# A decoder layer on one core: the order of work at the change of halves, in the fourth block's sums, at the first experts and at the load of the output weights

## The chip, the cores and the metric

The kernel runs on one core of a Trainium2 chip. Its time is the device time of one execution in microseconds (us). A core has five engines that run side by side, each working through its own queue in order: TensorE (PE in the profile; the loads of its weights are PEld), VectorE (DVE), ScalarE (ACT), GpSimd (POOL) and SyncE (SP), which here issues most DMA transfers. An engine waits for another by a semaphore. All data are float32.

## The reference, cut to what matters

The input x has 32 sequences of 64 tokens with 512 features, so 2048 tokens. Three residual blocks follow each other, each behind a layer norm.

```python
x = x + attn(layernorm(x))      # 32 heads of 128, within each sequence
x = x + cross(layernorm(x), ctx_1024)
x = x + ffn(layernorm(x))       # 64 experts, 8 chosen

# attn
q = rmsnorm(h @ Wq + bq, gq); k = rmsnorm(h @ Wk + bk, gk); v = h @ Wv + bv
o = softmax(q @ k.T / sqrt(128)) @ v          # per sequence and head
return o @ Wo + bo

# ffn
scores = softmax(h @ router_weight.T + router_bias)
w = top 8 of scores, zero elsewhere
return h * w.sum() + w @ expert_bias
```

Most of the work is in the four large products with Wq, Wk, Wv (512 x 4096 each) and Wo (4096 x 512).

## The kernel before, in words

**Tokens.** The 2048 tokens are 16 tiles of 128, 8 pairs of tiles, 4 quads of 2 pairs, and 2 halves of 2 quads. The attention goes through half 0 with all 16 groups of two heads, then through half 1. The variable `n` counts the 32 steps; `n = 16` is the change of halves, `n = 17` the second step of half 1.

**Strassen-like block products.** A product with the weights is split into 2 x 2 blocks and done with seven block products instead of eight. The seven left factors of a pair of tiles are called by number: 1 is a11, 2 is a12, 4 is a22, and 5, 6, 7, 3 are the sums s1 = a21 + a22, s2 = s1 - a11, s3 = a11 - a21, s4 = a12 - s2. `AttentionInput` makes them: `turn_first` turns the first tile of the pair on TensorE (L273) and copies a11 and a12 out of PSUM (L364, L365); `turn_second` turns the second, copies a22 (L372) and makes the sums s3 (L375), s1 (L376), s2 (L378) and s4 (L383).

**The first step of a half** (`hg == 0`) is done by `single`, one unit (a quad) after the other. `HeadGroup.project` issues the block products for q and k in the order 1, 2, 6, 5, 7, 4, 3, with those of the values (L440, `values`) between them; where `fifth_ahead` is set, as for the first unit of all, 5 comes ahead of 6. Products 1, 6, 7 and 4 add up in one PSUM bank (`pa`), 5 and 3 in another (`pb`), 2 in a third (`pc`); VectorE reads a bank (L513, L518) before the next product may add to it. `single` runs other work at numbered places between the products: `between[2]` is the place after the first product of the values, and so on. The line "turned probabilities" (`line.turn`) is at place 7. At `n = 0` the turning of the next inputs is at places 7 and 12, at `n = 16` at 6 and 11.

**All other steps** are done by `double`: a `Window` computes two units at once, with the scheme applied a second time inside each block, so that there are 7 x 7 products (L717). Its left factors are the token sums of `inner_input`: for each of the seven blocks `o`, two sums on VectorE (L393, L394), then two on GpSimd (L396, L397). They are made in steps 0 and 1 of each half. `Window.project` goes through four groups of blocks, (1, 5), (2, 6), (7, 3) and (4), each in four parts; the dictionary `more` puts work behind part (n, m). Behind parts (2, 1) to (3, 2) the window itself adds up parts of q and k on GpSimd for its first unit and on VectorE for its second (`add`, L797), and takes squares of them on ScalarE (L407). ScalarE also copies the values out of their bank (`keep`, L456), and the next product of the values adds to that bank.

**What sets the order.** TensorE's order is the program's order. In the attention that of VectorE, ScalarE and GpSimd is too. SP's order, and in the tail (from the output product on) that of VectorE, ScalarE and GpSimd, is set by a planner from its own costs. So an edit of the program moves an instruction on TensorE for certain, and on SP only where the planner follows.

**The fetches.** Behind a window ScalarE writes the inverse roots of the mean squares to DRAM (row writes, L684), and SP fetches them back, spread over all partitions (`rs`, L595), for the scaling of q and k on GpSimd and VectorE (L604, L606).

**The output product** (L911) needs Wo in four quarters; `load_wo` loads them (L883), the first into a buffer that the last but one step's weights held, issued in the program ahead of the last window.

**The tail** runs the rest of the layer for each tile (`cross_attention`, then `experts`) piece by piece between the output products of the following pairs; a generator's `yield w` says how many steps of the output products to let pass. `experts` ends with two products with the expert biases, one for each tile (L1283), added to x on VectorE (L1285), and the store of the result. They, like the output products, take their PSUM banks from `ps_a`, which has three. The next x tiles are loaded into the buffers of those that were stored, and GpSimd adds the bias to them (L899).

Of the kernel before, what the change touches and what calls it, by code (L numbers as in the profile page):

```python
# [24 lines left out]
NPAIR = NT // 2  # L25
# [16 lines left out]
def decoder_layer(  # L42
# [23 lines left out]
    nc = tc.nc  # L66
# [143 lines left out]
    first = const.tile([P, 1], F32, tag="first", name="first")  # L210
# [96 lines left out]
    class AttentionInput:  # L307
# [39 lines left out]
        def turn_first(self, copy=None, pool=None, tag="ps"):  # L347
            copy = copy or nc.scalar.copy
            pair = self.pair
            self.turned(pool or ps_s, tag)  # L350
            half, t, j = pair // 4, pair // 2 % 2, pair % 2
            if pair % 4 == 0:


                halves_x[half] = {o: block(f"x{o}_{half}") for o in (1, 2, 6, 5, 7, 3, 4)}
            raw = {
                o: it[:, 0 : 8 * P].rearrange("p (c t j n) -> p c t j n", c=2, t=2, j=2)
                for o, it in halves_x[half].items()
            }
            if j == 0:  # L360
                quads[pair // 2] = {o: it[:, :, t, :, :] for o, it in raw.items()}
            self.parts = [raw[o][:, :, t, j, :] for o in range(1, 8)]
            a11, a12 = self.parts[0:2]
            copy(a11, self.pt[0][:, 0:2, :])  # L364
            copy(a12, self.pt[0][:, 2:4, :])  # L365

        def turn_second(self):
            pair = self.pair
            self.turned(ps_s, "ps")
            pt = self.pt  # L370
            a11, a12, s4, a22, s1, s2, s3 = self.parts
            nc.scalar.copy(a22, pt[1][:, 2:4, :])  # L372
            first = pair < 2
            if not first:
                nc.vector.tensor_tensor(s3, a11, pt[1][:, 0:2, :], ALU.subtract)  # L375
            nc.vector.tensor_tensor(s1, pt[1][:, 0:2, :], a22, ALU.add)  # L376
            yield
            (nc.vector if first else nc.gpsimd).tensor_tensor(s2, s1, a11, ALU.subtract)  # L378
            yield
            if first:  # L380
                nc.vector.tensor_tensor(s3, a11, pt[1][:, 0:2, :], ALU.subtract)
                yield
            nc.gpsimd.tensor_tensor(s4, a12, s2, ALU.subtract)  # L383
            if pair in (NPAIR // 2, NPAIR // 2 + 1):
                coming.append(AttentionInput(pair + 2))

    inner_x = {}

# [824 lines left out]
    def experts(t, xt):  # L1213
        name = f"f{t}"
        xn = layernorm(xt, name)
        yield 3
        if t % 2 == 0:
            fts = work.tile([P, 2, KC, P], F32, tag="att", name=f"ft_{name}", bufs=1)
        else:
            fts, x_a, xn_a = chosen_by.pop(t - 1)  # L1220
        ft = fts[:, t % 2, :, :]
        nc.scalar.copy(ft, transposed(xn.rearrange("p (kc k) -> p kc k", k=P), name))
        yield 1
        if t % 2 == 0:
            chosen_by[t] = fts, xt, xn
            return
        tiles = [(t - 1, x_a, xn_a), (t, xt, xn)]

        plt = ps_s.tile([P, P], F32, tag="ps", name=f"plt_{name}")
        for kc in range(KC):  # L1230
            for side in range(2):
                nc.tensor.matmul(
                    plt[side * NEXP : (side + 1) * NEXP, :],
                    rwt[:, kc, :],
                    fts[:, side, kc, :],
                    start=kc == 0,
                    stop=kc == KC - 1,
                )
        lgt = work.tile([P, P], F32, tag="wt", name=f"lgt_{name}")
        nc.scalar.copy(lgt, plt)  # L1240
        yield 0
        pl = ps_s.tile([P, 2, NEXP], F32, tag="ps", name=f"pl_{name}")
        nc.tensor.transpose(pl.rearrange("p a e -> p (a e)"), lgt, ident)
        n = len(tiles)
        lgs = work.tile([P, n, NEXP], F32, tag="lg", name=f"lg_{name}")
        nc.vector.tensor_tensor(
            lgs, pl, rb_b.unsqueeze(1).to_broadcast([P, n, NEXP]), ALU.add
        )
        wds = work.tile([P, n, NEXP], F32, tag="wds", name=f"wds_{name}")
        for side, (at, x_, xn_) in enumerate(tiles):  # L1250
            lg = lgs[:, side, :]
            top = small.tile([P, 8], F32, tag="top", name=f"top{side}_{name}")
            nc.vector.max(top, lg)
            neg = small.tile([P, 1], F32, tag="neg", name=f"neg{side}_{name}")
            nc.vector.tensor_scalar(neg, top[:, 0:1], -1.0, None, ALU.mult)
            ex = work.tile([P, NEXP], F32, tag="ex", name=f"ex{side}_{name}")
            den = small.tile([P, 1], F32, tag="den", name=f"den{side}_{name}")
            nc.scalar.activation(ex, lg, AF.Exp, bias=neg, accum_out=den)
            inv = small.tile([P, 1], F32, tag="inv1", name=f"inv1{side}_{name}")
            nc.vector.reciprocal(inv, den)  # L1260

            rest = work.tile([P, NEXP], F32, tag="rest", name=f"rest{side}_{name}")
            nc.vector.match_replace(rest, top, lg, -3e38)
            chosen = work.tile([P, NEXP], F32, tag="chosen", name=f"chosen{side}_{name}")
            nc.vector.tensor_tensor(chosen, lg, rest, ALU.not_equal)
            wd = wds[:, side, :]
            nc.vector.scalar_tensor_tensor(wd, ex, inv, chosen, ALU.mult, ALU.mult)
            ws = small.tile([P, 1], F32, tag="ws", name=f"ws{side}_{name}")
            nc.vector.tensor_reduce(ws, wd, AX.X, ALU.add)

            nc.vector.scalar_tensor_tensor(x_, xn_, ws, x_, ALU.mult, ALU.add)
        yield 2
        n *= NEXP
        pw = ps_t.tile([P, P], F32, tag="pt", name=f"pw_{name}")
        nc.tensor.transpose(pw[0:n, :], wds.rearrange("p a e -> p (a e)")[:, 0:n], ident)
        wt = work.tile([P, P], F32, tag="wt", name=f"wt_{name}")
        nc.scalar.copy(wt[0:n, :], pw[0:n, :])
        yield 1

        pms = [ps_a.tile([P, D], F32, tag="pa", name=f"pm{i}_{name}") for i in range(len(tiles))]  # L1280
        for i, pm in enumerate(pms):
            rows = slice(i * NEXP, (i + 1) * NEXP)
            nc.tensor.matmul(pm, wt[rows, :], eb_sb[rows, :], start=True, stop=True)  # L1283
        for (at, it, _), pm in zip(tiles, pms):
            nc.vector.tensor_tensor(it, it, pm, ALU.add)  # L1285
            nc.sync.dma_start(out=out_flat[bass.ts(at, P), :], in_=it)
# [178 lines left out]
    coming = []  # L1465
# [141 lines left out]
    for n, (hg, half) in enumerate(groups):  # L1607
        w = weights.pop(n)
        units = [HeadGroup(hg, 2 * half + t, w) for t in range(2)]
        prepare(n)  # L1610
        if hg == 0:
# [4 lines left out]
            }  # L1616
            if n > 0:
                half_two = [coming.pop(0).turn_second() for _ in range(2)]
                between[2] = lambda: [list(it) for it in half_two]
            else:  # L1620

                rest = [it.turn_second() for it in first_two]
                between[1] = lambda: w_0.one_sum(nc.vector, 5)
                between[2] = lambda: (
                    [next(it) for _ in range(2) for it in rest],
                    w_0.one_sum(nc.vector, 6),
                    [next(it) for it in rest],
                )
                between[4] = lambda: (
                    w_0.one_sum(nc.gpsimd, 4),  # L1630
                    w_0.one_sum(nc.gpsimd, 7),
                    [next(it, None) for it in rest],
                )
                for at in (11, 6):
                    between[at + 1] = between.pop(at)
                units[0].fifth_ahead = True
# [26 lines left out]
        else:  # L1663
# [7 lines left out]
            def also(n, m, it):  # L1671
                more.setdefault((n, m), []).append(it)

            if hg == 1:
                for at, o in (
                    ((0, 0), 2),
                    ((0, 1), 6),
                    ((0, 1), 3),
                    ((1, 0), 7),
                    ((1, 1), 3),  # L1680
                    ((1, 2), 4),
                    ((2, 2), 4),
                ):
                    also(*at, lambda o=o: inner(o))
            if half == 0 and 2 <= hg < 2 + NT // 2:
# [12 lines left out]

            if n + 1 == len(groups):
                four = four_blocks("wo_0")  # L1700
                wo_b = [[load_wo(0, 0, four[0:2], nc.sync)], []]
                also(1, 0, lambda: wo_b[1].append(load_wo(1, 0, four[2:4], nc.scalar)))
                a_0 = [[None, None], [None, None]]

# [84 lines left out]
    a12 = drain()  # L1789
# [110 lines left out]
```

## Time and profile before

| | us |
|---|---|
| median of 3 runs | 1857.03 |
| runs | 1856.47 to 1858.2 |
| the profiled execution | 1858.04 |
| its span (first to last instruction) | 1856.3 |
| TensorE busy | 1840.5 |
| GpSimd busy | 1009.6 |
| VectorE busy | 1248.4 |

The granted clock of TensorE was 1.00. In the timeline a row has the start of a group of equal instructions in us from the span's start, the time from its start to its end in us, engine, line, operation, what is written and what is read, shapes and count. In brackets behind it stand the idle time of the engine just before, and what ended it. The view of waits has: who waited at which line, for whom; us in total, how often, the longest. A matmul here is recorded as two, and its recorded duration reaches over the start of the next, since matmuls overlap; 128x256 ones start 0.216 us apart.

### The profile page before, as it was taken

The page shows a single profiled execution, that of the slowest core. Times are in us where ns is not written, and L with a number is a line of the kernel's source. Part 1 is how long each engine was busy: PE and PEld are TensorE (multiplying, and loading weights), DVE is VectorE, ACT ScalarE, POOL GpSimd, SP SyncE. Part 2 cuts the span into 40 slices and gives each one's busy share as a digit, 9 for nine tenths or more (in the row PEclk, how much of TensorE's full clock was granted, in tenths as well). Part 3 has the DMA queues.
Part 4 walks back from the last instruction along what each step waited for, and adds up shares of the span by engine and source line. Part 5 has one row for each costly group of instructions (what it writes and reads, how often), then busy time and mean ns, then how long its engine had stood idle before and what let it go on. Part 6 is the DMA issues. An engine that isn't in the chain of part 4 may idle for free.

```text
span 1856.3 us, 40645 instructions
## 1 busy us (share of the span) xinstructions
PE 1840.5 (99%) x16892; PEld 1606.4 (87%) x16892; DVE 1248.4 (67%) x2112; ACT 653.3 (35%) x1583; POOL 1009.6 (54%) x850
## 2 busy tenths in 40 slices
PE   9999999999999999999999999999999999999998
PEld 8889889998899888899889988988888788888876
DVE  7767787776677768777677777777684444544455
ACT  3343444344433443434443344344412112211222
POOL 4966777776667639777666776776242211211120
PEclk9999999999999999999999999999999999999999
DMA  4244434433443343333344333333945221233100
GB/s 143 70 138 148 127 122 131 126 109 117 131 132 115 115 138 115 104 115 103 117 133 129 115 115 109 110 104 123 297 134 193 94 102 61 83 105 109 54 26 23
DMA packets 164937, 215.06 MB, mean 116 GB/s; under 512 B 10192, under 2 KB 135696, under 8 KB 160656
## 3 DMA queue, kind: packets, MB, share of 16 engines
q1 hardware_dynamic: 157648, 206.36, 34.6%
q10 hardware_dynamic: 7104, 6.10, 1.0%
q8 instruction: 133, 2.18, 0.5%
q14 instruction: 52, 0.43, 0.1%
HBM read 172.05 MB, written 40.37 MB: 114 GB/s over the span
## 4 chain that ended last, share of the span: by engine, by line
PE 90%; DVE 3%; DMA 3%; POOL 3%; issue 1%; ACT 0%; SPq 0%; DVEq 0%; POOLq 0%; ACTq 0%
PE p_w L717 33%; PE py L911 20%; PE va L440 11%; PE vb L440 8%; PE o L654 3%; PE s L617 3%; PE ms_w L853 3%; PE pt_p L273 1%; PE pa L498 1%; PE e_x L1140 1%; PE py_x L1156 1%; PE pt_x L273 1%; POOL w L133 1%; DMA wo<-in_wo_dram 1%; PE py_x L1151 1%
## 5 line engine op out<-in xcount | busy, mean ns | idle before, releaser
L717 PE MATMUL p_w<-x,w 128*128 128x256 f32 x2940 | 721.4, 382 | 3.7 <-POOL x L396 1.6
L717 PEld LDWEIGHTS p_w<-x,w 128*128 128x128 f32 x2940 | 522.2, 191 | 60.0 <-POOL x L396 1.8
L440 PEld LDWEIGHTS va<-w,x 128*128 128x128 f32 x2048 | 268.6, 192 | 13.1 <-issue 0.3
L728 DVE TENSOR_TENSOR qk<-p_w,qk 128x512 f32<-128x512 f32 x360 | 213.4, 600 | 93.9 <-PE p_w L717 90.7
L456 ACT COPY v<-va 128x256 f32<-128x256 f32 x256 | 96.0, 375 | 496.5 <-PE va L440 496.5
L440 PE MATMUL va<-w,x 128*128 128x128 f32 x2048 | 270.0, 275 | 0.0
L741 DVE TENSOR_TENSOR qk<-p_w,qk 128x512 f32<-128x512 f32 x360 | 219.9, 620 | 41.1 <-PE p_w L717 37.7
L133 POOL TENSOR_TENSOR w<-w 128x768 f32<-128x768 f32 x124 | 244.3, 1982 | 2.4
L289 POOL TENSOR_TENSOR prob<-prob,inv 128x512 f32<-128x512 f32 x64 | 79.7, 1246 | 296.1 <-DVE inv L288 280.0
L604 POOL TENSOR_TENSOR qk<-qk,rs 128x512 f32<-128x512 f32 x128 | 174.2, 1361 | 115.4 <-DMA rs<-row_w 105.3
L911 PE MATMUL py<-wo,a 128*128 128x256 f32 x992 | 227.1, 382 | 0.0
L407 ACT ACTIVATE sq<-qk 128x512 f32<-128x512 f32 x256 | 161.4, 631 | 181.5 <-DVE qk L741 65.9
L911 PEld LDWEIGHTS py<-wo,a 128*128 128x128 f32 x992 | 184.1, 190 | 33.2 <-issue 8.9
L440 PEld LDWEIGHTS vb<-w,x 128*128 128x128 f32 x1536 | 201.5, 192 | 9.6
L440 PE MATMUL vb<-w,x 128*128 128x128 f32 x1536 | 202.4, 275 | 0.0
L606 DVE SCALAR_TENSOR_TENSOR qk<-qk,gqk,rs 128x512 f32<-128x512 f32 x128 | 175.6, 1372 | 5.0 <-DMA rs<-row_w 5.0
L911 PE MATMUL py<-wo_t,a 128*128 128x256 f32 x672 | 155.0, 382 | 0.0
L911 PEld LDWEIGHTS py<-wo_t,a 128*128 128x128 f32 x672 | 124.8, 190 | 19.2 <-issue 2.4
L1035 POOL TENSOR_TENSOR x<-x,p 128x256 f32<-128x256 f32 x42 | 40.7, 991 | 163.1 <-ACT p L1088 73.3
L460 DVE TENSOR_TENSOR v<-vb,v 128x256 f32<-128x256 f32 x192 | 80.9, 421 | 55.5 <-ACT v L456 29.4
L797 POOL TENSOR_TENSOR qk<-qk 128x256 f32<-128x256 f32 x120 | 102.9, 858 | 10.6 <-DVE qk L741 5.8
L281 DVE TENSOR_REDUCE mx<-s 128x8 f32<-128x512 f32 x64 | 44.1, 690 | 86.0 <-PE s L617 86.0
(253 smaller groups left out, 2228.3 us busy)
## 6 DMA issues: line engine op xcount, KB each, us to landing
rs<-row_w SPq DMA_DIRECT2D x120, 512.0 KB
mixed<-ot SPq DMA_DIRECT2D x64, 512.0 KB
a<-mixed SPq DMA_DIRECT2D x32, 1024.0 KB
w<-in_wq_dram SPq DMA_DIRECT2D x64, 256.0 KB
w<-in_wk_dram SPq DMA_DIRECT2D x62, 256.0 KB
w<-in_wv_dram SPq DMA_DIRECT2D x62, 256.0 KB
x<-in_x_dram SPq DMA_DIRECT2D x20, 256.0 KB
rs<-row SPq DMA_DIRECT2D x8, 512.0 KB
```

The costliest lines, as they stand in the source:

```text
L133: on.tensor_tensor(*(it.rearrange("p c j d -> p (c j) d") for it in (out, a, b)), ALU.subtract)
L407: nc.scalar.activation(sq, of, AF.Square)
L440: nc.tensor.matmul(to[:, j, :], left[i][:, c, j, :], right[i][:, c, 2, :], start=first and j == 0 and c == 0, stop=c == 1, skip_group_chec ...
L456: nc.scalar.copy(self.v[h, ab], what)
L460: nc.vector.tensor_tensor(it, what, it, ALU.add)
L604: nc.gpsimd.tensor_tensor(k, k, rk, ALU.mult)
L606: lambda: nc.vector.scalar_tensor_tensor(q, q, gqk, rq, ALU.mult, ALU.mult)
L717: nc.tensor.matmul(bank[:, s, :], self.w.inner[o][i], inner_x[self.half, o][i], start=first and s == 0, stop=True, skip_group_check=True,)
L728: nc.vector.tensor_tensor(to(t, j), bank, add(t, j), ALU.add)
L741: nc.vector.tensor_tensor(to(t, j), bank, to(t, j), ALU.add)
L797: on.tensor_tensor(to, to, what, ALU.add)
L911: nc.tensor.matmul(py, a[:, g, :], b[g // KH][:, g % KH, :], start=n == 0 and g == 0, stop=n == last and g == NHG - 1,)
```

## The change

It has five parts.

1. In `turn_first` the copy of a12 is always made by ScalarE; where pairs 4 and 5 are turned ahead of half 1, VectorE made it.
2. For pairs 4 and 5 `turn_second` now works as it did for pairs 0 and 1: s1 first, then s2 on VectorE instead of GpSimd, then s3, with s4 alone left to GpSimd; three steps at place 2 of the unit, the last at place 4. The loads of the following pairs are asked for at its beginning. The first unit of half 1 takes product 5 ahead of product 6.
3. The GpSimd sums of block 4 (L396, L397) go from behind part (2, 2) of the window to behind part (2, 0), in both halves.
4. The first pair of tiles' expert products (t = 1) come one step sooner.
5. The first load of the output weights goes from ahead of the last window to behind its part (0, 3), in the program.

```diff
             copy(a11, self.pt[0][:, 0:2, :])
-            copy(a12, self.pt[0][:, 2:4, :])
+            nc.scalar.copy(a12, self.pt[0][:, 2:4, :])
...
-            first = pair < 2
+            first = pair % 4 < 2
+            if pair in (NPAIR // 2, NPAIR // 2 + 1):
+                coming.append(AttentionInput(pair + 2))
...
             nc.gpsimd.tensor_tensor(s4, a12, s2, ALU.subtract)
-            if pair in (NPAIR // 2, NPAIR // 2 + 1):
-                coming.append(AttentionInput(pair + 2))
...
-        yield 1
+        yield 0 if t == 1 else 1
         pms = [ps_a.tile([P, D], F32, tag="pa", name=f"pm{i}_{name}") for i in range(len(tiles))]
...
                 half_two = [coming.pop(0).turn_second() for _ in range(2)]
-                between[2] = lambda: [list(it) for it in half_two]
+                between[2] = lambda: [next(it) for _ in range(3) for it in half_two]
+                between[4] = lambda: [next(it, None) for it in half_two]
+                units[0].fifth_ahead = True
...
-                    ((2, 2), 4),
+                    ((2, 0), 4),
...
-                wo_b = [[load_wo(0, 0, four[0:2], nc.sync)], []]
+                wo_b = [[], []]
+                also(0, 3, lambda: wo_b[0].append(load_wo(0, 0, four[0:2], nc.sync)))
```

## The prediction

> **What bounds the kernel now.** I read the page first, then the waits of TensorE, then the timeline of each place where it waits.
>
> ```profile
> PE 1840.5 (99%) x16892; PEld 1606.4 (87%) x16892; DVE 1248.4 (67%) x2112; ACT 653.3 (35%) x1583; POOL 1009.6 (54%) x850
> ```
>
> TensorE is busy for 99% of a span of 1856.3 us and the change removes no matmul. So it can win only idle time of TensorE, about 16 us, start and end included. The view of waits names it:
>
> ```profile
> PE s L617 <- POOL qk L604: 1.9, 3, 1.1
> PE p_w L717 <- POOL x L396: 1.6, 1, 1.6
> ...
> PE p_w L717 <- DVE qk L728: 1.3, 1, 1.3
> PE pm_f L1283 <- DVE x L1285: 0.8, 1, 0.8
> ...
> PE pa L498 <- DVE x L364: 0.7, 1, 0.7
> ...
> PE pa L498 <- POOL x L378: 0.6, 1, 0.6
> ```
>
> Five of these rows are what the change touches: L364 and L378 (change of halves), L396 (token sums of the fourth block), L1285 (first experts) and L728 (which waits for a fetch beside the first load of the output weights). Measured from one matmul's start to the next, less the usual spacing, they cost 0.91, 0.79, 1.74, about 1.0 and 1.50 us. All of it together is 5.9 us or 0.32%. The question is which wait comes next at each place.
>
> **1. Change of halves.** TensorE and then VectorE:
>
> ```profile
> 672.41 2.00 PE L498 MATMUL pa<-x,w 128*128 128x256 f32 x8 [0.74 <-DVE x L364]
> ...
> 679.41 2.00 PE L498 MATMUL pa<-x,w 128*128 128x256 f32 x8 [0.62 <-POOL x L378]
> ...
> 684.73 0.60 PE L273 MATMUL pt_p<-ident,prob 128*128 128x128 f32 x4
> 685.17 1.89 PE L498 MATMUL pa<-x,w 128*128 128x256 f32 x8
> ```
> ```profile
> 681.44 0.69 DVE L513 TENSOR_TENSOR qk<-pa,bqk 128x512 f32<-128x512 f32 x1 [2.19 <-PE pa L498]
> ```
>
> (a) Two of four copies go from VectorE to ScalarE. The first product needs the third of the old four (671.94 to 672.35). It can now run as soon as its transposes end at 671.66, so at 671.70 to 672.12: product one starts 0.24 us sooner. The moved copies stand behind ScalarE's store of the mixture, which ends at 673.13. They end at about 673.7, and the second product needs them at 675.76: hidden by the first product, the values and the transposes.
>
> (b) Product six waited for s2 on GpSimd. Product five, which needs only s1 (VectorE, by 676.8), takes its place, so the 0.79 us go: it starts at 678.38. s2 is now on VectorE: two operations of 0.42 us where GpSimd's were 0.73. VectorE has six operations before the sum for product two instead of four, and that sum ends at about 678.9. Its square waits a little, and TensorE doesn't wait for it. s4 is done by 679 and is needed at 690.
>
> (c) What is late next: products six and seven write the same bank, and VectorE must read six (L513, 0.69 us) before seven may add to it. Before, the values, a transpose and product five (together 3.5 us) lay between. Now only the turned probabilities do (0.44 us). In the first half the same reordering moves the turning of the next inputs to this place; here that is not done. By the rows: six starts at 681.87 and ends at 683.76; VectorE then takes 0.03 + 0.69 us; seven starts at 684.53 instead of 684.04, and a restart costs 0.10 more. After seven TensorE stands at 686.36 where it stood at 686.90. Net of (a) to (c): **0.54 us won** of 1.70. Bounds: 0.3 (if VectorE is late with pair six's sums) and 1.03 (if seven doesn't wait).
>
> (d) On SP the fourth of the coming inputs falls behind two fetches, about 1 us later. Its transposes are at 690.4, more than 10 us after, so it is hidden. The two fetches gain 0.4 us or so; who waits for them (GpSimd's and VectorE's scaling) is not waited for by TensorE here.
>
> **2. Fourth block's token sums.** TensorE, GpSimd, ScalarE in the second half:
>
> ```profile
> 752.90 1.05 PE L440 MATMUL va<-w,x 128*128 128x128 f32 x8
> 755.52 1.13 PE L717 MATMUL p_w<-x,w 128*128 128x256 f32 x4 [1.57 <-POOL x L396]
> 756.49 1.05 PE L440 MATMUL va<-w,x 128*128 128x128 f32 x8
> ```
> ```profile
> 751.28 3.33 POOL L797 TENSOR_TENSOR qk<-qk 128x256 f32<-128x256 f32 x4
> 754.57 0.91 POOL L396 TENSOR_TENSOR x<-x 128x256 f32<-128x256 f32 x1
> 755.55 0.73 POOL L397 TENSOR_TENSOR x<-x 128x256 f32<-128x256 f32 x1
> ```
> ```profile
> 753.84 0.63 ACT L407 ACTIVATE sq<-qk 128x512 f32<-128x512 f32 x1 [3.19 <-POOL qk L797]
> 754.64 0.63 ACT L407 ACTIVATE sq<-qk 128x512 f32<-128x512 f32 x1 [0.17 <-POOL qk L797]
> 755.18 0.35 ACT L456 COPY v<-va 128x256 f32<-128x256 f32 x1
> ```
>
> GpSimd is full: it ran without a gap from 741.7. The change puts L396 and L397 ahead of the four L797 in the same queue, so the six end where they ended, at about 756.2, and it is the L797 that are late, by 1.65 us. Two chains hang on them. The second L797 releases VectorE's L728 (0.42 us), which frees the bank for product six: 754.5 + 0.42 gives 755.0, against 755.52. So this wait shrinks only by 0.5 us. The third and fourth release two squares on ScalarE, and behind these, in its queue, stands the copy L456 of the values. In the row above that copy starts at 755.18 although the matmuls it reads ended at 753.95. The next value product (756.49) may not write before it has read. After the change: fourth L797 ends 756.15, second square starts 756.18, copy 0.54 us later (755.18 less 754.64), 0.35 to 0.37 us long, then 0.05: the value product starts at 757.12 instead of 756.49. With a restart of 0.07 that is **0.70 us lost**, not 1.74 won. Bounds: 1.74 won (if the copy is not held up), 1.0 lost (if the L797 take the 0.9 us that the slowest took).
>
> A rule bears on this. The Trainium skill, SBUF — State Buffer, section Who interferes with whom: a VectorE instruction with two inputs in SBUF and a GpSimd one that reads it exclude each other, and the later one blocks fully. The rows show less: L797 on GpSimd took 0.91 us beside VectorE's own L797 and 0.73 alone, though a full block until 751.60 would have added 0.32. The moved L396 and L397 now stand beside those two VectorE sums. By the rows the loss is 0.70; with full blocks about 0.2 more, 0.90. I take the rows.
>
> First half: at the same place GpSimd has slack (L396 ended 86.17, needed 87.01), so nothing is there to win. Moved ahead, the fourth L797 ends at 86.9 instead of 85.2, the copy at 87.86 instead of 87.58, and the value product at 87.88 waits to 87.91: **0.1 us lost** with its restart, bounds 0 and 0.3.
>
> **3. First experts.**
>
> ```profile
> 1473.33 1.12 PE L1283 MATMUL pm_f<-eb_sb,wt_f 64*128 64x512 f32 x2
> 1475.23 1.12 PE L1283 MATMUL pm_f<-eb_sb,wt_f 64*128 64x512 f32 x2 [0.78 <-DVE x L1285]
> ```
>
> The second product takes the bank of the first, because the two before it are still held by output products whose sums come later on VectorE. Moved four output matmuls and the energies ahead (to 1470.3), the pair keeps that order: first product, VectorE's sum (0.69 us; VectorE idles there too), second product. The weights are ready at 1468.52. The wait moves and stays: 0. What follows is sooner or hidden: the stores and the next two x loads start some 3.5 us earlier; the energies and their softmax come 3 us later, ready near 1480 with their transposes at 1486.31. Bounds: 0.9 won, 0.3 lost.
>
> **4. Output weights.** SP's queue is not in the program's order; a planner sets it. In the compiled order of both kernels the two loads stand at the same place: behind the mixture's store, ahead of the row writes and all four fetches. So nothing moves, and the 1.50 us stay. It is 0.
>
> **Sum.** -0.54 + 0.70 + 0.10 + 0 + 0 = **+0.26 us** on the profiled span of 1856.3, with 1.74 us around it (1858.04). That execution lies 1.0 us above the median of 1857.03; the difference put on the median gives **1857.3 us**.
>
> **Rivals.**
> - *The sums' wait really goes.* If the squares on ScalarE do not hold the copy, -0.54 - 1.74 gives 1854.8 us. For it: the view of waits names L396 alone. Against: three queues in order, shown above.
> - *All that is named is won*, 0.91 + 0.79 + 1.74 + 0.9 = 4.3 us, 1852.7; with the fetch too, 1851.2. Against: steps 1c, 3 and 4.
> - *Slower: VectorE is held at the first experts.* Its compiled order now has the sum L1079 ahead of the two softmax normalisations. It waits for GpSimd's L899, which waits for an x load (row: landed 2.65 us after its issue at 1477.87). Issued near 1474.1 it lands near 1476.8 and holds nothing. From a landing past 1482 (8 us) the transposes at 1486.31 are late, us for us; 3.7 us lost needs a landing near 1486. Then 1861 us.
> - *No part does anything* gives 1857.0, inside the forecast.
>
> **Chances.** The forecast 0.72 (own range 1856.3 to 1858.3), the first rival 0.16, the second 0.05, the third 0.07. 0.2% is 3.7 us, about what a measurement of this kernel can tell from no change. Faster by more: 0.06 (second rival and a little of the first). Slower by more: 0.03, as the third rival mostly stays below that. Within: 0.91. The range runs from near the first rival to the forecast with its losses at their bounds and a run's scatter of 0.9 us: 1854.9 to 1858.9.
>
> **What would show it.** Right: before the second product seven at the change of halves a wait of about 0.4 us for L513; no wait for L396, but one of about 1.1 us of the value product for the copy L456 near 757; 0.8 us at the experts and 1.3 us at L728 unchanged. Wrong: squares before which GpSimd is done by 754.7, or a wait of VectorE for L899 that TensorE feels.

## The result: 2.8 us slower, less than two parts in a thousand

| | median | lowest to highest | runs |
|---|---|---|---|
| before | 1855.59 us | 1853.96 to 1858.2 | 18 |
| after | 1858.54 us | 1856.7 to 1861.01 | 18 |

The ratio is 1.0015, with an interval from 1.0008 to 1.0022: 1.5 to 4.1 us slower. The forecast of 1857.3 us stood for +0.26 us. That the change would move the time by less than 0.2% was right (the interval just reaches 0.22%); the small loss is real and ten times the forecast, and most of it came from a place that the forecast did not look at.

The profiled execution after took 1859.26 us, its span is 1857.4 us. The page's first part, as before, shows an engine that is never short of work:

```profile
PE 1839.4 (99%) x16892; PEld 1605.3 (86%) x16892; DVE 1244.6 (67%) x2112; ACT 653.8 (35%) x1585; POOL 1007.8 (54%) x848
```

The waits of TensorE after (what waited, for what; us in total, times, longest):

```profile
PE p_w L717 <- DVE qk L728: 3.9, 4, 1.6
...
PE e_x L1140 <- ACT prob_x L1186: 1.4, 1, 1.4
PE va L440 <- ACT v L456: 0.8, 1, 0.8
PE pm_f L1284 <- DVE x L1286: 0.8, 1, 0.8
...
PE pa L498 <- DVE x L364: 0.5, 1, 0.5
...
PE pa L498 <- DVE qk L513: 0.3, 1, 0.3
```

The waits for L378 and for L396 are gone. New are L513 (0.3) and L456 (0.8), which the forecast named, L728 at the window of the fourth block's sums (one of the four), and a wait of the energies' product L1140 for a softmax (1.4), which it did not. To see where time is lost and won I laid TensorE's start times of the two profiles side by side, matmul by matmul, and noted where the difference steps:

| place (us after) | step | what |
|---|---|---|
| 672 to 686 | -0.51 | change of halves |
| 755 to 757 | +0.68 | token sums, second half |
| 88 | +0.19 | token sums, first half |
| 1468 to 1476 | -0.40 | first experts |
| 1785 to 1788 | +1.89 | the last pair of cross attention: L1140 waits for the softmax L1186 |
| up to 22 | -1.17 | the first loads |
| 111 to 203 | +0.95 | L728, which waits for a fetch |
| 1243 to 1365 | -0.52 | L728, L853 and L617, at fetches |

The first five rows add to +1.85 us, and all eight to +1.1, by which the spans differ. The last three are at places whose own instructions stand as before. The experiments below show that four of the first five repeat from kernel to kernel with their edits; the step at 88 varies, and the last three rows come and go.

At the change of halves (TensorE, in order of time: start, duration, line, idle time before it and what ended it):

```profile
672.16 1.99 PE L498 MATMUL pa<-x,w 128*128 128x256 f32 x8 [0.52 <-DVE x L364]
...
681.87 1.89 PE L498 MATMUL pa<-x,w 128*128 128x256 f32 x8
683.60 0.60 PE L273 MATMUL pt_p<-ident,prob 128*128 128x128 f32 x4
684.55 1.99 PE L498 MATMUL pa<-x,w 128*128 128x256 f32 x8 [0.35 <-DVE qk L513]
686.38 1.05 PE L440 MATMUL vb<-w,x 128*128 128x128 f32 x8
```

Product six starts at 681.87 and seven at 684.55, where the forecast had 681.87 and 684.53. In the second half's window, on TensorE and then on ScalarE:

```profile
754.62 1.13 PE L717 MATMUL p_w<-x,w 128*128 128x256 f32 x4 [1.16 <-DVE qk L728]
756.56 1.16 PE L440 MATMUL va<-w,x 128*128 128x128 f32 x8 [0.82 <-ACT v L456]
```
```profile
754.82 0.63 ACT L407 ACTIVATE sq<-qk 128x512 f32<-128x512 f32 x1 [4.68 <-POOL qk L797]
755.62 0.63 ACT L407 ACTIVATE sq<-qk 128x512 f32<-128x512 f32 x1 [0.18 <-POOL qk L797]
756.16 0.35 ACT L456 COPY v<-va 128x256 f32<-128x256 f32 x1
```

Two squares wait for GpSimd's late L797, the copy of the values stands behind them, and the value product behind the copy.

The place that was missed is the last pair, some 1100 us after anything that was edited except the output weights and the experts. TensorE there, before and then after:

```profile
1786.10 1.16 PE L1140 MATMUL e_x<-kvs,xn_x 64*128 64x128 f32 x16
```
```profile
1785.36 0.49 PE L1140 MATMUL e_x<-kvs,xn_x 64*128 64x128 f32 x2
1787.26 1.16 PE L1140 MATMUL e_x<-kvs,xn_x 64*128 64x128 f32 x14 [1.41 <-ACT prob_x L1186]
```

And VectorE, before and then after:

```profile
1783.35 0.42 DVE L1046 TENSOR_TENSOR x<-x,py 128x256 f32<-128x256 f32 x1
```
```profile
1784.39 0.42 DVE L1046 TENSOR_TENSOR x<-x,py 128x256 f32<-128x256 f32 x1 [1.73 <-POOL x L899]
1784.72 0.95 DVE L1182 TENSOR_SCALAR neg_x<-mx_x 128x4 f32<-128x4 f32 x2
```

Before, L1046 waited for nothing. L899 on GpSimd adds the output bias to an x tile when its load has landed. L1182, behind L1046 on VectorE, starts the softmax, and the next energies need the bank that the softmax reads.

### The profile page after: what moved, and what is told of

The parts are those of the page before. It is cut to its first block, busy times and chain, and to the rows that moved or that the text cites. A ratio compares the mean times of both kernels' runs of the same rounds, so it can differ in the third digit from the quotient of the medians.

```text
span 1857.4 us, 40648 instructions
## 1 busy us (share of the span) xinstructions
PE 1839.4 (99%) x16892; PEld 1605.3 (86%) x16892; DVE 1244.6 (67%) x2112; ACT 653.8 (35%) x1585; POOL 1007.8 (54%) x848
## 4 chain that ended last, share of the span: by engine, by line
PE 90%; DVE 4%; POOL 2%; DMA 2%; issue 1%; ACT 0%; SPq 0%; DVEq 0%; POOLq 0%; ACTq 0%
PE p_w L717 33%; PE py L911 19%; PE va L440 11%; PE vb L440 8%; PE o L654 3%; PE s L617 3%; PE ms_w L853 3%; PE pt_p L273 1%; PE pa L498 1%; PE e_x L1140 1%; PE py_x L1156 1%; PE pt_x L273 1%; POOL w L133 1%; PE py_x L1151 1%; DMA rs<-row_w 1%
## 5 line engine op out<-in xcount | busy, mean ns | idle before, releaser
L717 PE MATMUL p_w<-x,w 128*128 128x256 f32 x2940 | 721.4, 382 | 4.5 <-DVE qk L728 3.9
L717 PEld LDWEIGHTS p_w<-x,w 128*128 128x128 f32 x2940 | 521.4, 190 | 61.4 <-DVE qk L728 4.7
L728 DVE TENSOR_TENSOR qk<-p_w,qk 128x512 f32<-128x512 f32 x360 | 213.1, 600 | 97.4 <-PE p_w L717 92.7
L456 ACT COPY v<-va 128x256 f32<-128x256 f32 x256 | 96.1, 375 | 492.9 <-PE va L440 492.6
L604 POOL TENSOR_TENSOR qk<-qk,rs 128x512 f32<-128x512 f32 x128 | 172.7, 1350 | 121.0 <-DMA rs<-row_w 106.4
L606 DVE SCALAR_TENSOR_TENSOR qk<-qk,gqk,rs 128x512 f32<-128x512 f32 x128 | 166.4, 1300 | 6.9 <-DMA rs<-row_w 6.9
L797 POOL TENSOR_TENSOR qk<-qk 128x256 f32<-128x256 f32 x120 | 102.8, 858 | 10.5 <-DVE qk L741 5.8
```

The costliest lines, as they stand in the source:

```text
L456: nc.scalar.copy(self.v[h, ab], what)
L604: nc.gpsimd.tensor_tensor(k, k, rk, ALU.mult)
L606: lambda: nc.vector.scalar_tensor_tensor(q, q, gqk, rq, ALU.mult, ALU.mult)
L717: nc.tensor.matmul(bank[:, s, :], self.w.inner[o][i], inner_x[self.half, o][i], start=first and s == 0, stop=True, skip_group_check=True,)
L728: nc.vector.tensor_tensor(to(t, j), bank, add(t, j), ALU.add)
L797: on.tensor_tensor(to, to, what, ALU.add)
```

## The experiments

Theories. **A**: each step is as the forecast has it, and the rest is the chance of when fetches land. **B**: the edit at the experts costs in the last pair. **C**: the token sums cost in the first half too. After the first four runs **D** and **E** took the place of B and C: code fetches.

### One part at a time

The change of halves alone (all of the diff but its last three places), the token sums alone, the experts alone, and everything but the token sums:

```diff
# sums alone
-                    ((2, 2), 4),
+                    ((2, 0), 4),
# experts alone
-        yield 1
+        yield 0 if t == 1 else 1
# everything but the sums: the changed kernel with
-                    ((2, 0), 4),
+                    ((2, 2), 4),
```

Halves:

> The change of halves alone, everything else as before. Theory A (each step as the prediction has it, the rest of the measured +2.8 us from the moments at which fetches land): -0.5 us against the kernel before, with TensorE's three waits of 0.9 (L364), 0.8 (L378) and none replaced by 0.7, none and 0.4 (L513). Theory B (the first experts' edit is what costs, at the last pair): the same -0.5. Theory C (the token sums' edit is what costs, in the first half too): the same -0.5. If instead this kernel is slower than before by 1 us or more, all three are wrong and the loads that this part moves on SP are to be looked at.

Sums:

> The fourth block's token sums alone at their new place. Theory A: +0.8 us (0.70 in the second half at the value product near 757, 0.10 in the first near 88). Theory B: the same +0.8. Theory C: about +2.0, the 1.2 more in the two later windows of the first half, where L728 waits for a fetch (near 119 and 203 us in the kernel after). The first rival (the sums' wait really goes) would give -1.7.

Experts:

> The first experts alone with their product sooner. Theory A: between 0 and -0.4 us (the energies' matmuls run inside the wait, as the trace after showed), and at the last pair nothing beyond chance. Theory B: -0.4 at the experts and +1.7 at the last pair near 1787 (the energies' product waits for the softmax, which waits for the x load through L899 and L1046), +1.3 in all. Theory C: as A.

All but the sums:

> The changed kernel with the fourth block's token sums back at their old place. Theory A: -0.5 to -0.9 us against the kernel before. Theory B: +0.8 (all but the halves' 0.5 of the tail's loss stays). Theory C: -0.5 to -0.9. The wait for L396 of 1.6 us near 755 is back, the one for the copy L456 gone.

Measured against the kernel before (1856.19 us, 49 runs), with the steps of TensorE's start times at the edited places and in the last pair:

| | median | ratio (interval) | edited place | last pair |
|---|---|---|---|---|
| halves | 1856.92 | 1.0006 (1.0 to 1.0013) | -0.51 | **+2.08** |
| sums | 1858.12 | 1.0009 (1.0001 to 1.0018) | +0.67, +0.18 | 0 |
| experts | 1854.87 | 0.9994 (0.9986 to 1.0003) | -0.40 | 0 |
| all but sums | 1856.68 | 1.0003 (0.9994 to 1.0011) | -0.51, -0.40 | **+1.39** |

B falls: the experts alone are a gain, and the last pair doesn't stall. The stall is in the two kernels that hold the change of halves. All three theories had that part at -0.5 us; it measures +1.1 by the ratio, and its own place shows -0.51. So it loses at 1786 what it wins at 680, and more. C falls too: the wait of 0.8 us for L728 near 119 is in the experts alone, whose instructions up to there are those of before, and not in the sums alone. It is before's own profile that happened not to have it.

### What links 680 us to 1786 us

In the two kernels the instructions of the last pair stand in the same order as before, on every engine. What differs lies in between. I set five moments of the last pair against the start of the sixteen matmuls of the energies just before the stall (0; 1779.63 us before, 1778.89 after):

| us | code fetch, 8 KB | first store issued | x loads issued | first L899 |
|---|---|---|---|---|
| before | -2.42 to -2.10 | -2.28 | -0.24 | 2.30 |
| sums | -2.49 to -1.98 | -2.28 | -0.25 | 2.71 |
| experts | -2.48 to -2.03 | -2.28 | -0.24 | 2.60 |
| halves | -1.37 to -0.73 | -2.00 | +0.47 | 4.39 |
| all but sums | -1.37 to -0.80 | -2.00 | +0.33 | 3.70 |
| after | -1.33 to -0.76 | -2.00 | +0.43 | 4.20 |

The stream of instructions is itself fetched over the DMA engines; the page lists these as queues of the kind "instruction". By counting how many instructions each engine had executed at each fetch of that queue, this one belongs to SP: it came when SP had executed 975 in the three rows above, and 978 in the three below. (ScalarE's stream has another length in the three kernels below too, but its next piece comes only 30 us later, near 1808.) The change of halves moves a load on SP past two fetches, and behind it, at 712 us, one instruction that only waits ahead of a fetch (L595) is gone. The trace has 1000 instructions of SP in place of 1001, so every later block of its code begins, and is fetched, one instruction later in the work. In all six rows the fetch begins about 1.0 us after SP's 975th instruction ends (1.05 before, 1.02 after). That one used to be a load of the context, ahead of the wait for the finished x tile, and the fetch came while SP stood at that wait, before the store; now it is the wait itself, and the fetch comes about 1.1 us later, beside the store. SP issues the store 0.3 us later, though its wait ends at the same moment; the x loads, which go into the stored tiles, are issued 0.6 to 0.7 us later; the first L899, which waits for them, starts 1.0 to 2.1 us later.

The DMA view of the first microsecond from the store's issue, before and then after (queue, kind: packets, MB, share of 16 engines):

```profile
q1 hardware_dynamic: 26, 0.05, 14.3%
```
```profile
q1 hardware_dynamic: 26, 0.05, 14.3%
q14 instruction: 1, 0.01, 3.6%
```

The stores start alike, with 26 packets, and after there is one piece of code among them. What is late is their end: the last of the 256 packets of the two stores starts 2.32 us after the first store's issue before, and 2.77 us after. So in the kernel after the x load is 0.67 us late: 0.28 from the store's later issue and 0.39 from the time that passes from there to the x load.

The larger part comes behind that. From the x load's issue (SPq) to the first L899 on GpSimd it is 2.54 us before and 3.77 after, 1.23 us more:

```profile
1779.39 1.16 SPq L187 DMA_DIRECT2D x<-in_x_dram  x2
1781.93 1.39 POOL L899 TENSOR_TENSOR x<-x,bo_b 128x512 f32<-128x512 f32 x1 [3.04 <-DMA x<-in_x_dram]
```
```profile
1779.32 1.13 SPq L187 DMA_DIRECT2D x<-in_x_dram  x2
1783.09 2.49 POOL L899 TENSOR_TENSOR x<-x,bo_b 128x512 f32<-128x512 f32 x2 [4.94 <-DMA x<-in_x_dram]
```

This is theory D. It has a rival, E: TensorE's own code comes in pieces of 16 KB on another queue, and one piece falls near the x loads, 0.7 to 0.8 us after their issue in the stalled kernels and 2.0 to 2.4 after it in the others. Each theory was meant to act alone: with three more idle transposes at the very start (TensorE's stream longer, SP's as it was), or with SP's stream made one instruction shorter or longer.

```diff
# before, with 31 idle transposes
-    for i in range(28):
+    for i in range(31):
# halves alone, SP's stream one longer
-    load(bvt, bv_t)
+    load(bvt[0 : P // 2, :], bv_t[0 : P // 2, :])
+    load(bvt[P // 2 : P, :], bv_t[P // 2 : P, :])
# before, SP's stream one shorter
-    load(bvt, bv_t)
+    load_beside(bvt, bv_t)
```

`load_beside` issues on ScalarE's queue.

> The kernel before with 31 in place of 28 idle transposes at the start (L1484), so that TensorE's stream has three matrix instructions more and each block of its code is fetched a little earlier in the work; SP's stream is unchanged. Theory D (the stall of 0.9 to 1.6 us in the last pair, seen in the three kernels that hold the change of halves and in none of the others, comes from SP's code: the change takes one waiting instruction out of SP's stream, so the 8 KB of its next code are fetched among the packets of the store ahead of the x loads instead of before them): no stall here, SP's code is fetched about 2.4 us before the energies' matmuls (L1140) near 1780, the x loads are issued 0.24 us before these, time 0 to +0.1 us. Theory E (TensorE's own code, 16 KB a piece, which in those three kernels is fetched 0.7 to 0.8 us after the first x load's issue and not 2.0 to 2.4): the fetch comes near 0.8 us after that issue, L899 starts over 1 us later, and a stall of 0.9 to 1.6 us before L1140 near 1786 appears: +1 to +1.6 us.

> The change of halves alone, with the small load of the value bias split into two of half the partitions at the start, so that SP's stream has again as many instructions as before the change; TensorE's stream is as in the change of halves alone. Theory D: SP's code is again fetched about 2.4 us before the energies' matmuls near 1778 and ahead of the store's packets, the x loads are issued 0.24 us before these matmuls and not 0.3 to 0.5 after, the stall of 1.6 us near 1786 is gone: -0.5 us against the kernel before where the change of halves alone gave +0.7 to +1.1. Theory E: the stall stays, +0.7 to +1.1.

> The kernel before with the small load of the value bias issued by ScalarE and not by SP, so that SP's stream has one instruction less, as with the change of halves; nothing else is changed. Theory D: a stall of 0.9 to 1.6 us appears before L1140 near 1786, with SP's code fetched about 1.35 us before the energies' matmuls and the x loads issued 0.3 to 0.5 after their start: +0.9 to +1.6 us. Theory E: no stall, no difference.

| | median | ratio (interval) | SP's instructions | code fetch | x loads issued | last pair |
|---|---|---|---|---|---|---|
| before, 31 transposes | 1855.59 | 0.9998 (0.9989 to 1.0006) | 1001 | -2.49 | -0.22 | 0 |
| halves, SP one longer | 1855.93 | 0.9996 (0.9988 to 1.0004) | 1001 | -2.49 | -0.22 | 0 |
| before, SP one shorter | 1862.07 | 1.003 (1.0019 to 1.0041) | 1000 | -1.36 | +0.47 | **+1.69** |

(before: 1856.3 us, 35 runs.) The change of halves without the stall, and the kernel before with it: TensorE there, in these two, and VectorE in the second:

```profile
1783.82 1.16 PE L1140 MATMUL e_x<-kvs,xn_x 64*128 64x128 f32 x16
```
```profile
1788.07 0.49 PE L1140 MATMUL e_x<-kvs,xn_x 64*128 64x128 f32 x2
1789.77 1.16 PE L1140 MATMUL e_x<-kvs,xn_x 64*128 64x128 f32 x14 [1.21 <-ACT prob_x L1186]
```
```profile
1786.90 0.42 DVE L1046 TENSOR_TENSOR x<-x,py 128x256 f32<-128x256 f32 x1 [1.53 <-POOL x L899]
```

Sixteen matmuls in one row, with no idle time, where the halves alone had two, a wait of 1.60, and fourteen. And the kernel before, with nothing changed but which queue loads a small tile once at the start, gets the stall. D holds: SP's stream alone brings the stall and takes it away. E is not the cause: the last kernel's TensorE stream is that of before, and it stalls, and the halves' TensorE stream does not stall with SP's old length. (The longer TensorE stream says little. Its 16 KB piece still came 2.28 us after the x load's issue, 2.04 before, and not the 0.8 that was meant.) But TensorE's piece is probably a link of the chain. In the six stalled kernels it starts 0.6 to 1.0 us behind the late x load's issue, and L899 starts 1.4 to 1.7 us after the piece ends; in the eight others the piece starts only 0.5 to 0.7 us ahead of L899. That reads as if the late load's packets queue behind it, and would be the 1.23 us. It follows SP's shift, since it came early even where TensorE's stream was untouched (1.06 us after the zero of the table against 1.80 before). No run moves this piece alone, so this link is not shown.

The kernel with SP's stream one shorter loses 5.6 us by the ratio, not the 0.9 to 1.6 that was expected. Its profile has the stall and two more losses, +2.0 us by 25 us (the first loads), and +1.7 at 1367 (the scores wait 2.21 us for a scaling by L604), though that one only makes up for a wait of before near 1313 that it lacks (-1.6). Whether the load's new queue causes the first was not tried.

The Trainium skill (Runtime: NRT & Kernel Launch, Instruction fetch mechanics) says that a sequencer fetches its next block of code through a DMA queue of its own while it executes, and that this is mostly hidden. The rows agree in part: SP loses only the 0.3 us before the store. By that rule the stall would be about 0, and it measures 1.4 to 2.1 us, as the data transfers beside and behind the fetch land later.

### The whole change without the stall

```diff
# the changed kernel with
-    load(bvt, bv_t)
+    load(bvt[0 : P // 2, :], bv_t[0 : P // 2, :])
+    load(bvt[P // 2 : P, :], bv_t[P // 2 : P, :])
```

> The whole changed kernel with the value bias loaded in two halves, so that SP's stream has its old length again. If the last pair's stall is all that SP's code fetch cost (theory D), 1.4 to 1.6 us less than the changed kernel: by the steps in the trace (-0.5 halves, +0.8 sums, -0.35 experts) about 0.0, by the medians (+2.8 less 1.5) about +1.3 us against the kernel before; no stall near 1787. If the changed kernel loses by something else too, it stays at +2 or more.

1856.93 us against 1856.22, ratio 1.0003 (0.9995 to 1.0011). No wait in the last pair. Its steps are -0.51, +0.67, +0.18 and -0.40: -0.05 us. So without that stall the change does about nothing; the forecast's +0.26 lies within the interval (-0.9 to +2.0 us).

### Why the token sums lose

The forecast said that GpSimd's full queue only hands the delay on, through L797, the squares and the copy. Two ways to cut that chain: take the sums off GpSimd, or let the copy go ahead of the squares.

```diff
# the changed kernel; second half, fourth block only
-        nc.gpsimd.tensor_tensor(s2, s1, x11, ALU.subtract)
-        nc.gpsimd.tensor_tensor(s4, x12, s2, ALU.subtract)
+        on = nc.vector if (half, o) == (1, 4) else nc.gpsimd
+        on.tensor_tensor(s2, s1, x11, ALU.subtract)
+        on.tensor_tensor(s4, x12, s2, ALU.subtract)
```

> The changed kernel with the fourth block's last two sums of the second half on VectorE in place of GpSimd (0.42 us each there by L383's rows), at the place where the change has them. If my step 2 is right that GpSimd's full queue only hands the delay on: the wait for L396 is gone and GpSimd's four L797 are no later than before, so the copy L456 isn't held and the value product doesn't wait; L728 comes up to 0.84 us later behind the two sums, so about 0.4 us of wait remain: some 1.3 us won near 755 against before, 2.0 against the changed kernel, so about -0.8 to +0.8 us against before, the last pair's stall still in it. If the rival is right that the wait there is not of GpSimd's making, the waits near 755 stay near 2 us in sum.

1858.88 us against 1856.3, ratio 1.0014 (1.0006 to 1.0023), with the last pair's stall in it (+1.38). Near 755 the chain is gone as expected: no wait for L396, none for L456. But nothing was won, since the wait moved 6 us ahead. VectorE, GpSimd and TensorE of this kernel (its lines after 395 are one higher):

```profile
746.02 1.49 DVE L397 TENSOR_TENSOR x<-x 128x256 f32<-128x256 f32 x1
747.54 1.37 DVE L398 TENSOR_TENSOR x<-x 128x256 f32<-128x256 f32 x1
748.83 0.68 DVE L729 TENSOR_TENSOR qk<-p_w,qk 128x512 f32<-128x512 f32 x1
```
```profile
745.46 1.76 POOL L165 TENSOR_TENSOR w<-w 128x512 f32<-128x512 f32 x1
747.19 1.44 POOL L166 TENSOR_TENSOR w<-w 128x512 f32<-128x512 f32 x1
```
```profile
749.57 1.99 PE L718 MATMUL p_w<-x,w 128*128 128x256 f32 x8 [2.13 <-DVE qk L729]
```

My expectation had 0.42 us for each of the two sums on VectorE. They took 1.49 and 1.37, and each ended 0.28 to 0.29 us after the GpSimd instruction beside it (747.22 and 748.63). L729 behind them then frees TensorE's bank late. From 744 to 757 the kernel loses 0.74 us against before, as much as the change itself.

Then the order on ScalarE. A first attempt put the two squares one step later in the program:

```diff
                 (2, 3): lambda: (
                     add(1, 1, (1, 1), (0, 1)),
-                    squares(1, 0, 0),
-                    squares(1, 1, 0),
                 ),
-                (3, 0): lambda: add(1, 0, (1, 0), (1, 1)),
+                (3, 0): lambda: (
+                    squares(1, 0, 0),
+                    squares(1, 1, 0),
+                    add(1, 0, (1, 0), (1, 1)),
+                ),
```

> The changed kernel with the two squares of the window's third product (L407) put behind the copy of the values (L456) in ScalarE's queue, in both halves and all windows; the rest as in the changed kernel. By step 2 of the prediction: the value product near 757 no longer waits for L456 (0.8 us less), the token sums' edit turns from 0.7 us lost near 755 to some 0.1 us won, and the wait for L728 of 1.2 us stays; +2.0 us against the kernel before, the last pair's stall in it. If the copy isn't what holds the value product, it waits as long as before.

1858.34 us against 1856.22, ratio 1.0012 (1.0005 to 1.0019), and 0.82 us of wait for L456 as before. It tells nothing: the copy is issued at (3, 0), after these squares, so ScalarE's order did not change. A second attempt, on the better version described next, put them at (3, 1), in this window alone, and is told there.

### A better version

The parts that win, at the places that the runs speak for: the change of halves with the turning of the next inputs one product later, as the first half has it; the experts; the fourth block's sums where they were; the bias in two loads.

```diff
# the changed kernel with
                 units[0].fifth_ahead = True
+                for at in (11, 6):
+                    between[at + 1] = between.pop(at)
-                    ((2, 0), 4),
+                    ((2, 2), 4),
-    load(bvt, bv_t)
+    load(bvt[0 : P // 2, :], bv_t[0 : P // 2, :])
+    load(bvt[P // 2 : P, :], bv_t[P // 2 : P, :])
```

> A version made of what the runs speak for: the change of halves with the turning of the next inputs one product later, between six and seven, as in the first half; the first experts sooner; the fourth block's sums at their old place; the value bias in two loads, so that SP's stream keeps its length. By the steps: halves -0.5, product seven's wait for L513 gone -0.4, experts -0.35, no stall in the last pair: -1.3 us against the kernel before. If the turned inputs are not ready one place later, or the banks they are turned in are still held, the wait goes to them and it is -0.9 or worse.

1853.53 us against 1856.22, ratio 0.9985 (0.9978 to 0.9991): the best of all, faster than both kernels. The change of halves on TensorE:

```profile
680.46 1.89 PE L498 MATMUL pa<-x,w 128*128 128x256 f32 x8
682.19 0.60 PE L273 MATMUL pt_p<-ident,prob 128*128 128x128 f32 x4
682.62 1.04 PE L273 MATMUL pt_a<-ident,xn 128*128 128x128 f32 x8
683.50 1.89 PE L498 MATMUL pa<-x,w 128*128 128x256 f32 x8
```

Between products six and seven there are now 1.3 us of transposes, and seven doesn't wait. The change of halves is worth -1.12 us here, against -0.51. With the experts' -0.40 the edited places win 1.5 us, near the 1.3 expected; the ratio says 2.7 (1.7 to 4.1), and what is more has no edited place.

To this version the token sums' edit was added once more, with the two squares behind the copy in that window:

```diff
-                    squares(1, 0, 0),
-                    squares(1, 1, 0),
+                    hg != 1 and (squares(1, 0, 0), squares(1, 1, 0)),
...
                 (3, 1): lambda: (
+                    hg == 1 and (squares(1, 0, 0), squares(1, 1, 0)),
...
-                    ((2, 2), 4),
+                    ((2, 0), 4),
```

> The version made of what the runs speak for, with the fourth block's sums at the change's new place after all, but in that window (the second of each half) the two squares L407 of the third product behind the third copy L456 in ScalarE's queue; the run with the squares behind the copy had left the order of these three as it was, since the copy is issued one step later than I took it. By step 2 of the prediction: no wait of the value product for L456 near 754, a wait for L728 of about 1.2 us before it in place of 1.57 for L396, nothing in the first half: 0.4 us less than the version without this edit, which gave -2.7 us by the medians: about -3.1 us against the kernel before. If the late L797 hold something else (the square of the fourth product, the fourth copy behind it), a wait of up to 0.8 us stays near 756 to 758 and the gain is not there.

1854.19 us against 1856.37, ratio 0.9987 (0.9981 to 0.9994). TensorE and ScalarE in the window:

```profile
753.79 1.13 PE L717 MATMUL p_w<-x,w 128*128 128x256 f32 x4 [1.17 <-DVE qk L728]
754.76 1.05 PE L440 MATMUL va<-w,x 128*128 128x128 f32 x8
```
```profile
752.67 0.37 ACT L456 COPY v<-va 128x256 f32<-128x256 f32 x1 [3.35 <-PE va L440]
754.00 0.63 ACT L407 ACTIVATE sq<-qk 128x512 f32<-128x512 f32 x1 [0.96 <-POOL qk L797]
```

The copy runs as soon as its matmuls end, and the value product follows the wait for L728 at once. Against the version without the edit TensorE gains 0.41 us at this wait, as expected, but loses 0.22 again in the next part (L717 at 755.77, again behind VectorE's L728), so 0.20 remain. The edit loses 0.67 us with the old order on ScalarE and wins 0.20 with the new one: the copy behind the squares was what turned it into a loss. The medians of the two versions can't be told apart.

## Why the prediction was right, and what it missed

- **1a to 1c, change of halves: right.** -0.54 forecast, -0.50 to -0.51 measured in every kernel that holds it unshifted. Product one 0.23 us sooner (0.24), L378's wait gone (-0.89 with its restart), product seven at 684.55 (684.53) behind L513.
- **1d, the fourth load on SP: the step that failed.** "Hidden" was true for the load and its transposes. Not counted was what the move does to SP's stream as a list of instructions: one waiting instruction less, all later code fetched one instruction later in the work, and 1100 us on a stall of 1.4 to 2.1 us where an x load had little room. This cost +1.89 us in the profile after. The third rival had the mechanism (VectorE held by L899 at a late x load) at another place and for another reason.
- **2, token sums: right.** 0.70 lost forecast, 0.67 to 0.68 measured, by the path that was named: no wait for L396, one of 1.16 us for L728, and the value product at 756.56 behind the copy (757.12 in a count that started 0.5 us later). First half 0.1 forecast with bounds 0 and 0.3: 0.18 to 0.19 in three kernels, but 0 in the one with the first attempt at the squares and 0.66 in the one with the sums on VectorE, though both have the changed kernel's order of work up to there. What differs is how far GpSimd's work is behind: the second square starts 0.29 us behind the start of the value matmuls in the first of these two, 1.38 in the second and 0.90 in the changed kernel. So the forecast's +0.1 holds for one state of the queues. The first rival (the sums' wait really goes) is out.
- **The rule on VectorE and GpSimd.** I took the rows, which showed less than a full block. Here L396 and L397 took 0.92 and 0.85 us, 0.3 us over the lone 0.73 together, and the loss came out at 0.68, nearer to 0.70 than to the rule's 0.90. But where a VectorE sum began while a GpSimd one was under way, in the experiment with the sums moved to it, the full block of the Trainium skill (SBUF — State Buffer, Who interferes with whom) is what the rows show, and my 0.42 us a sum was wrong by a factor of three.
- **3, first experts: a term too small.** 0 forecast, -0.40 in each of the eight kernels that hold it. The wait of 0.78 us for L1286 did stay, as forecast. But the energies' product, which works on 64 rows like the experts' product, now stands behind it and runs in the same time:

```profile
1471.87 0.69 PE L1284 MATMUL pm_f<-eb_sb,wt_f 64*128 64x512 f32 x1 [0.78 <-DVE x L1286]
1471.88 0.71 PE L1140 MATMUL e_x<-kvs,xn_x 64*128 64x128 f32 x4
1472.41 0.59 PE L1284 MATMUL pm_f<-eb_sb,wt_f 64*128 64x512 f32 x1
```

  Four of its sixteen matmuls take no time of their own: 4 of 16 in 1.16 us are 0.29 of the 0.40 us.
- **4, output weights: no effect seen.** The wait for L728 near 1313 is 1.55 us after and 1.33 before, but between 0 and 0.90 in the other kernels without this edit and between 0 and 0.86 in the others with it. It follows the landing of a fetch.
- **The sum.** The four steps at edited places and the last pair give +1.85 us against +2.8 by the ratio, whose interval begins at 1.5. The remaining 0.9 us has no place of its own and is less than what single executions of one kernel differ by. That 1857.3 came within 1.3 us of the measured median is partly luck: it stood on a median of 1857.03 before, from 3 runs, where 18 runs give 1855.59, and 1858.54 still lies beyond the forecast's own range (to 1858.3) and only within the wide one. So is the sign: without the missed stall the steps add to -0.05 us, and the small loss was forecast for another reason than the one that made it.

## What to carry to other kernels

When a load or a wait is moved on a queue, compare the number of instructions on that engine before and after, the ones that only wait included. If it changed, look for transfers with no slack anywhere later, and where the code fetches fall beside them; a dummy instruction that restores the count tells a stall of this kind from one that belongs to the edit. And before work is moved ahead on a full engine, follow what it pushes back through the next two queues: the loss here sat in ScalarE's order, two engines away from the edit.

## What was not expected of the hardware

- One instruction more or less on SP moves a time by more than 1 us at a place 1100 us later: the six kernels with 1000 instructions of SP in their trace stall by 1.4 to 2.1 us in the last pair, and the eight others, with 1001, don't.
- Code is fetched over the DMA engines beside the data: SP's in pieces of 8 KB that took 0.3 to 0.6 us and TensorE's in pieces of 16 KB that took 0.9 to 1.5 us in the last pair.
- A VectorE sum of two 128x256 tiles in SBUF takes 0.42 us alone and 1.37 to 1.49 us when a GpSimd sum is under way.
